# Taking beta1 h from the transposed h on chip in an edge-gated graph layer

## The chip, the cores and the metric

The kernel runs on one core of one Trainium2 chip. The metric is the device time of one launch in microseconds (us), and the number quoted is the median of several launches. The engines are TensorE (PE, with its weight loads shown apart as PEld), VectorE (DVE), ScalarE (ACT), GpSimd (POOL) and SyncE (SP). SP, ACT and POOL issue transfers (DMAs), each from a queue of its own.

## What is computed

`x` holds 16 batches of 1024 nodes with 256 features in fp32; `adj` is a 1024 x 1024 matrix of which only about 0.9% (with the diagonal) is not zero. With h = x:

```python
pre_u = jnp.einsum('bud,dk->buk', h_t, W1[:d])
pre_v = jnp.einsum('bvd,dk->bvk', h_t, W1[d:])
hidden = relu(pre_u[:, :, None, :] + pre_v[:, None, :, :] + b1)
S = sigmoid(jnp.einsum('buvk,ko->buvo', hidden, W2)[..., 0] + b2[0])
a_t = jnp.einsum('buv,bud->bvd', S * A_a, h_t)
m_t = jnp.einsum('uv,bud->bvd', A_m, h_t) * h_t
z_t = beta1 * h_t + beta2 * (jnp.einsum('bvd,de->bve', a_t, Wa) + ba) + beta3 * (jnp.einsum('bvd,de->bve', m_t, Wm) + bm)
```

The last line is the one that matters here: every output row is beta1 times its own h plus two products with 256 x 256 weights.

## The kernel before

**Tables and blocks.** The 16 batches form four groups of four (`GB`). Each group has a table in device memory, one row for each node: 1024 values of pre_u and the 1024 values of h of its four batches, 8 KB in all. A block is one group with one tile of 128 target nodes, so there are 32 blocks. Their order is a list, `order`: group 0 with tiles 0 to 5, group 1 with tiles 0 to 5, group 0 with tiles 6 and 7, group 1 with tiles 6 and 7, then groups 2 and 3 with all eight tiles each. Block 24 is thus the first of the last group, and block 31 the last of all.

**Steps.** A block has ten steps, 320 in all; a step handles 128 edge slots. In each step:

- POOL gathers 128 table rows (1 MB) into one of eight buffers `fetched` (L518);
- PE expands pre_v of the targets to the edge slots (`pc`, L615, two products of 512 columns), and DVE adds it to the gathered pre_u (L648);
- DVE takes relu, multiplies by W2 and sums, once for each of four batches (L656), and ACT makes the sigmoid (L659) and scales the left-hand matrices (L661);
- PE sums the gathered h rows into the targets (`acc`, L673), after which the buffer is free for another gather.

The engines' order is written out by hand. The loop over steps issues `expand(n + 2)`, then `products(n, ...)`, then `add(n + 1)` and `gate(n)`; so the product of a step is issued two steps ahead of its use. `after(step, f)` puts a piece of work off to the end of a later step. All engines take their own instructions in this order.

**What is made beside the steps, inside `products`.** `halves` computes pre_v of the next block from its transposed h (`hT`, L445). `rows` computes pre_u rows of a later group, in half-rows of eight PE instructions, and stores them in the table; the steps at which this runs stand in `plan`. `turn_over` transposes the sums (L691), ACT copies them to `LT` (L694), and DVE multiplies the part that needs it by the transposed h (`times_h`, L705). In blocks 0 to 10 the edge lists of four later target tiles are also made, mostly by small DVE instructions that fill gaps (`lists`).

**The end of a block (`block_end`).** It runs within the following block, in steps 4 to 7 (from step 10 of the kernel on). It makes z in two halves of two batches each. For each half PE adds the bias row and eight products of 256 columns (L722) in PSUM, ACT copies the sum to a part of `LT` that is no longer needed (L736), and one step later DVE computes hb = hb * beta1 + z (L737); SP stores it to `out` (L739). hb is a tile `h_blk` (four buffers) into which SP loads h of the two batches from the table, in steps 5 and 7 of the block itself (L921). In the last group's second halves DVE isn't used: PE adds beta1 times the identity (`be1_eye`) times hb to the sum (L726), and ACT copies it to hb (L728).

**The transposed h.** A tile `hT` of 512 KB holds the transposed h of one block. Eight such tiles circulate in a list `hT_free`, three more from step 110 on; a few loads use two other tiles (`hta`). `drop_hT` returns a tile to the list. Before the change this happens after the second `times_h` of the block, at step 3 of the following block. The loads of `hT` are issued by SP at the steps in `plan`: for groups 2 and 3 in step 56 + 10 i and 136 + 10 i, for the second loads of group 1 in step 37 + 10 i.

Of the kernel before, what the change touches and what calls it, by code (L numbers as in the profile page):

```python
# [7 lines left out]
FP = mybir.dt.float32  # L8
# [3 lines left out]
ALU = mybir.AluOpType  # L12
AX = mybir.AxisListType
P = 128
# [3 lines left out]
def kernel(  # L18
# [42 lines left out]
    nc = tc.nc  # L61
    B, N, D = x.shape
    NT = N // P
    DC = D // P
    GB = 4
    NG = B // GB
    GD = GB * D
    W = 64
    NW = P // W
    TW = 5  # L70
    E = TW * P
# [9 lines left out]
    const = ctx.enter_context(tc.tile_pool(name="const", bufs=1))  # L81
# [94 lines left out]
    ident = fixed([P, P], "ident")  # L176
# [32 lines left out]
    big = main.enter_context(tc.tile_pool(name="big", bufs=2))  # L209
# [3 lines left out]
    lst = ExitStack()  # L213
    lists_done = lst.close
    lst = lst.enter_context(tc.tile_pool(name="lst", bufs=1))
# [26 lines left out]
    def lists(vt):  # L242
# [49 lines left out]
        first = R[:, 1:2]  # L292
# [34 lines left out]
        nc.vector.tensor_tensor(thr[:, vt:vt + 1], last, none, ALU.add)  # L327
        yield "op"
        RR = lst.tile([P, NW, RC], FP, name="RR", bufs=2)
        few = lst.tile([P, E], mybir.dt.uint8, name="few", bufs=2)  # L330
        yield "slot"
        for w, mine in enumerate((soon, late)):
            nc.vector.tensor_scalar(RR[:, w, :], R, mine, None, ALU.mult)
# [68 lines left out]
    def after(step, f):  # L402
        due.setdefault(step, []).append(f)
# [19 lines left out]
    def drop_hT(k):  # L423
        del hTs[k]
        if k in hT_of:
            hT_free.append(hT_of.pop(k))
# [77 lines left out]
            pass  # L504

    T = TW * NW

    BS = NG * NT

# [89 lines left out]
    def scale_late():  # L599
        nc.vector.tensor_scalar(ba_b, ba_b, be2, None, ALU.mult)  # L600
        nc.vector.scalar_tensor_tensor(bias, bias, be3, ba_b, ALU.mult, ALU.add)
        spread(bias_p, bias)
        nc.vector.tensor_scalar(w_a, w_a, be2, None, ALU.mult)
        nc.vector.tensor_scalar(w_m, w_m, be3, None, ALU.mult)
        hT_free.append(spare_)

# [19 lines left out]

    running = []
    be1_eye = []  # L630

    def piece_of(r, n):

# [49 lines left out]
    def turn_over(k, w, q, step):  # L683
        if w == 0 and q == 0:
            LTs[k] = one.tile([P, GB, 2, DC, P], FP, name="LT")
        LT = LTs[k]
        pt = small("pt").rearrange("p (r k c v) -> p r k c v", r=2, c=DC, v=V)
        ev = evs.pop(q)
        for i in range(4):
            r, c = divmod(i, DC)  # L690
            nc.tensor.transpose(pt[:, r, :, c, :], ev[:, r, c * P:(c + 1) * P], ident)  # L691
        v = slice(w * W + q * U, w * W + (q + 1) * U)
        r = (w * W + q * U) // V
        nc.scalar.copy(LT.rearrange("p b k c (r v) -> p r (b k c) v", v=V)[:, r:r + 2],  # L694
                       pt.rearrange("p r k c v -> p r (k c) v"))
        apart = k == BS - 1 and w == NW - 1
        if not apart:
            if not q:
                return
            v = slice(w * W, (w + 1) * W)  # L700

        def times_h():
            m = LT.rearrange("p (b two) k c n -> p b (two k c) n", two=2)[:, :, DC:3 * DC, v]
            h = hTs[order[k]].rearrange("p (b two) c n -> p b (two c) n", two=2)[:, :, :, v]
            nc.vector.tensor_tensor(m, m, h, ALU.mult)  # L705
            if w == NW - 1 and q == 1:
                drop_hT(order[k])
        after(step + (1 if k == BS - 1 or w else 2), times_h)

    def block_end(k):  # L710

        g, vt = order[k]
        hb = hbs[k]
        for h in range(2):
            for i, wt in ((1, w_a), (0, w_m)):
                step = yield
                if i:
                    pz = small("pz")
                    add_row(pz, bias_p)
                for bb in range(2):  # L720
                    for c in range(DC):
                        nc.tensor.matmul(pz[:, bb * D:(bb + 1) * D], LTs[k][:, 2 * h + bb, i if bb else 1 - i, c, :], wt[:, c, :],  # L722
                                         start=False, stop=(i == 0 and c == DC - 1), skip_group_check=True)
            if h == 1 and g == NG - 1:
                for bb in range(2):
                    nc.tensor.matmul(pz[:, bb * D:(bb + 1) * D], be1_eye[0], hb[h][:, bb, :], start=False, stop=True,  # L726
                                     skip_group_check=True)
                nc.scalar.copy(hb[h], pz.rearrange("p (b d) -> p b d", b=2))  # L728
                b = g * GB + 2 * h
                after(step + 2, lambda hb=hb[h], b=b: nc.sync.dma_start(  # L730
                    out[b:b + 2, vt * P:(vt + 1) * P, :].rearrange("b p d -> p b d"), hb))
                continue
            z = pz.rearrange("p (b d) -> p b d", b=2)
            if step >= ROOM:
                z = LTs[k][:, 2 * h].rearrange("p k c n -> p (k c n)").rearrange("p (b d) -> p b d", b=2)
                nc.scalar.copy(z, pz.rearrange("p (b d) -> p b d", b=2))  # L736
            after(step + 1, lambda hb=hb[h], z=z: nc.vector.scalar_tensor_tensor(hb, hb, be1, z, ALU.mult, ALU.add))  # L737
            b = g * GB + 2 * h
            after(step + 2, lambda hb=hb[h], b=b: nc.sync.dma_start(  # L739
                out[b:b + 2, vt * P:(vt + 1) * P, :].rearrange("b p d -> p b d"), hb))  # L740
        del hbs[k], LTs[k]

# [42 lines left out]
    def plan(blocks, ns):  # L787

        for k, (load, *pieces) in zip(blocks, ns):
            loads[load] = k  # L790
            at.update((n, k) for n in pieces)

    plan(turn[NT:], ((1, 2, 4), (2, 8, 9), (5, 12, 18), (10, 19, 22), (20, 28, 29), (23, 32, 38), (30, 39, 42), (40, 48, 49)))
    for g, first in ((2, 60), (3, 140)):
        plan([(g, vt) for vt in range(NT)], ((first - 4 + 10 * i, first + 8 + 10 * i, first + 12 + 10 * i)
                                             for i in range(NT)))
    plan([(1, vt) for vt in range(FIRST)], [(37 + 10 * i,) for i in range(FIRST)])
    plan([(g, vt) for g in range(2) for vt in range(FIRST, NT)], ((103,), (113,), (125,), (133,)))
    begun = set(turn[:NT])
    end = parts = piece = last = None  # L800
# [81 lines left out]
    for n in range(total + 2):  # L882
# [26 lines left out]
        if n == 1:  # L909
# [3 lines left out]
            be2 = load_rows(beta2, 1, "be2", nc.sync)  # L913
            be3 = load_rows(beta3, 1, "be3", nc.sync)
            after(10, scale_late)
        if s in (5, 7) and k < BS - 1:
            h = s // 7
            hb = big.tile([P, 2, D], FP, name="h_blk", bufs=4)
            hbs.setdefault(k, []).append(hb)
            g, vt = order[k]  # L920
            nc.sync.dma_start(hb.rearrange("p b d -> p (b d)"),  # L921
                              table[g][vt * P:(vt + 1) * P, GD + 2 * h * D:GD + (2 * h + 2) * D])
# [14 lines left out]
        if n == LISTS:  # L937
            assert not running and all(next(x, None) is None for x in made)
            lists_done()
            more = main.enter_context(tc.tile_pool(name="more", bufs=1))  # L940
            hT_free.extend(hT_places(more, MORE, NH))
            be1_eye.append(more.tile([P, P], FP, name="be1_eye"))
            nc.vector.tensor_scalar(be1_eye[0], ident, be1, None, ALU.mult)
        if n == 120:
            nc.gpsimd.partition_all_reduce(longest, rest, P, bass_isa.ReduceOp.max)
            after(n + 12, count_rest)
# [115 lines left out]
```

## Time and profile before

| quantity | value |
|---|---|
| median of 3 launches | 1077.57 us (1075.32 to 1079.38) |
| profiled launch, own time | 1082.24 us |
| its span, first to last instruction | 1080.4 us |
| PE busy (7673 matmuls) | 1020.1 us |
| DVE busy | 1017.6 us |
| ACT busy | 862.6 us |
| POOL busy | 459.3 us |
| bytes moved by DMA | 394.56 MB, mean 365 GB/s |

The page lists instructions in groups: the line of the source, the engine, the operation, what is written and read, how many there are; then the time in which at least one of them ran, the mean of one in ns, and the idle time of the engine ahead of them with what ended it. The groups that belong to the end of a block, from the list with shapes kept apart:

```profile
L722 PE MATMUL misc<-w_m,LT 128*128 128x256 f32 x496 | 117.3, 379 | 0.0
...
L737 DVE SCALAR_TENSOR_TENSOR h_blk<-h_blk,be,LT 128x512 f32<-128x512 f32 x55 | 40.9, 744 | 0.0
...
L736 ACT COPY LT<-misc 128x512 f32<-128x512 f32 x55 | 32.0, 582 | 29.1 <-PE misc L722 25.6 <-PE pc L615 1.4 <-issue 1.0
...
L726 PE MATMUL misc<-h_blk,be_eye 128*128 128x256 f32 x28 | 7.2, 379 | 0.0
```

PSUM tiles of 512 columns that change owners often carry the name `misc` there. Matmuls overlap, so the mean of one (379 ns) is longer than the time from one to the next (117.3 us for 496 of them). And the transfers:

```profile
h_blk<-table SPq DMA_DIRECT2D x62, 256.0 KB
out_dram<-h_blk SPq DMA_DIRECT2D x62, 256.0 KB
hT<-in_xT_dram SPq DMA_DIRECT2D x28, 512.0 KB
```

In views of windows each row gives a stretch of time, its length, the busy time and number of instructions of PE, PEld, DVE, ACT and POOL, the granted clock of PE, the busy share of the DMA engines and what they moved. In the chain of waits and in the timeline each row begins with the start and the length in us.

### The profile page before, as it was taken

To read this page: it belongs to the slowest core of one execution; us is meant where nothing else is said; L and a number is where in the kernel's file an instruction comes from. 1 tells how busy PE (TensorE), PEld (TensorE's weight loads), DVE (VectorE), ACT (ScalarE), POOL (GpSimd) and SP (SyncE) were. 2 spreads that over 40 slices of the span, in tenths; PEclk is the share of its full clock that TensorE was granted. 3 is DMA by queue.
4 is the path that set the end of the run, shared out by engine and by line. 5 is a ranking of instruction groups with operands and counts; after the bars stand their busy time and mean duration, and the time that the engine had idled before them with its cause. 6 is when DMAs were issued, how large, how long until landed. Compare 5 with 4: busy or idle time off the path is not lost.

```text
span 1080.4 us, 24120 instructions
## 1 busy us (share of the span) xinstructions
PE 1020.1 (94%) x7673; PEld 731.3 (68%) x7673; DVE 1017.6 (94%) x3481; ACT 862.6 (80%) x2616; POOL 459.3 (43%) x456
## 2 busy tenths in 40 slices
PE   7777999999999999999999999999999999999996
PEld 6654676776666776677777767777766667666654
DVE  8687999998999999999999999999999999999993
ACT  3246787788888887898888888889889889999983
POOL 2666676555257334553333334333333333333330
PEclk9989999999999999999999999999999999999999
DMA  9999899999999999999999999999999999999991
GB/s 283 327 340 385 313 339 381 362 382 378 403 352 371 408 381 385 379 403 395 404 393 399 412 384 392 408 396 389 381 361 370 369 348 368 365 381 369 365 341 44
DMA packets 147752, 394.56 MB, mean 365 GB/s; under 512 B 18224, under 2 KB 94512, under 8 KB 111408
## 3 DMA queue, kind: packets, MB, share of 16 engines
q0 software_dynamic: 50544, 301.16, 70.9%
q1 hardware_dynamic: 83776, 78.66, 22.9%
q10 hardware_dynamic: 13296, 13.11, 3.5%
q8 instruction: 63, 1.03, 0.4%
q14 instruction: 73, 0.60, 0.1%
HBM read 396.93 MB, written 50.33 MB: 414 GB/s over the span
## 4 chain that ended last, share of the span: by engine, by line
PE 40%; DVE 34%; issue 10%; ACT 8%; DMA 5%; POOL 2%; another core or an unknown queue 0%; POOLq 0%; DVEq 0%; ACTq 0%
DVE fetched L656 16%; DVE fetched L648 12%; PE acc L673 10%; PE misc L722 10%; PE misc L445 9%; PE pc L615 7%; DMA fetched<-table,uidx 3%; PE misc L691 2%; ACT left L661 2%; DVE LT L705 1%; ACT X L489 1%; PE misc L449 1%; DVE low L484 1%; DVE h_blk L737 1%; DMA hT__635<-in_xT_dram 1%
## 5 line engine op out<-in xcount | busy, mean ns | idle before, releaser
L518 POOL DMA_INDIRECT fetched<-table,uidx x320 | 339.4, 1061 | 529.0 <-PE acc L673 389.0
L656 DVE SCALAR_TENSOR_TENSOR fetched<-fetched,w_b 128x256 f32<-128x256 f32 x1280 | 478.0, 419 | 0.0
L648 DVE TENSOR_TENSOR fetched<-fetched,pc 128x1024 f32<-128x1024 f32 x320 | 387.7, 1212 | 29.9 <-PE pc L615 19.4
L661 ACT ACTIVATE left<-left,gt 128x32 f32<-128x32 f32 (+1 forms) x1280 | 299.6, 305 | 10.4
L673 PE MATMUL acc<-fetched,left 128*32 128x256 f32 x4096 | 273.4, 385 | 6.3 <-ACT gt L659 3.7
L615 PE MATMUL pc<-X,mark 128*128 128x512 f32 x640 | 243.7, 462 | 10.9 <-DVE fetched L648 9.3
L673 PEld LDWEIGHTS acc<-fetched,left 128*32 128x32 f32 x4096 | 127.6, 109 | 112.1 <-issue 29.1
L615 PEld LDWEIGHTS pc<-X,mark 128*128 128x128 f32 x640 | 105.4, 189 | 88.9 <-issue 41.6
L659 ACT ACTIVATE gt<-sc,b_b 128x4 f32<-128x4 f32 x320 | 95.9, 300 | 46.7 <-DVE fetched L656 37.5
L722 PE MATMUL misc<-w_m,LT 128*128 128x256 f32 x496 | 117.3, 379 | 0.0
L722 PE MATMUL misc<-w_a,LT 128*128 128x256 f32 x496 | 117.2, 379 | 0.0
L445 PE MATMUL misc<-w_v,hT 128*128 128x256 f32 x448 | 107.6, 383 | 0.0
L722 PEld LDWEIGHTS misc<-w_a,LT 128*128 128x128 f32 x496 | 93.8, 189 | 15.3 <-issue 0.4
L722 PEld LDWEIGHTS misc<-w_m,LT 128*128 128x128 f32 x496 | 93.8, 190 | 15.1
L625 ACT ACTIVATE left<-onehot,val 128x64 f32<-128x64 bf16 (+1 forms) x320 | 102.9, 322 | 0.0
L385 POOL DMA_INDIRECT val<-in_adjT_dram,vidx x80 | 87.2, 1090 | 34.4 <-issue 20.4
L656 DVE DVE_READ_ACCUMULATOR fetched<-fetched,w_b 128x1 f32 x1280 | 100.7, 79 | 0.0
L691 PE MATMUL misc<-ident,ev 128*128 128x128 f32 x512 | 79.5, 278 | 18.5 <-issue 7.0
L445 PEld LDWEIGHTS misc<-w_v,hT 128*128 128x128 f32 x448 | 86.4, 193 | 14.3
L691 PEld LDWEIGHTS misc<-ident,ev 128*128 128x128 f32 x512 | 60.7, 141 | 45.7 <-ACT ev L681 15.2
L482 ACT CAST X<-misc 128x512 fp32r<-128x512 f32 x64 | 37.1, 580 | 55.2 <-PE misc L445 48.0
L445 PE MATMUL misc<-w_u,hT 128*128 128x256 f32 x320 | 76.6, 386 | 4.0 <-issue 3.8
(185 smaller groups left out, 1011.3 us busy)
## 6 DMA issues: line engine op xcount, KB each, us to landing
h_blk<-table SPq DMA_DIRECT2D x62, 256.0 KB
out_dram<-h_blk SPq DMA_DIRECT2D x62, 256.0 KB
hT<-in_xT_dram SPq DMA_DIRECT2D x28, 512.0 KB
table<-in_x_dram ACTq DMA_DIRECT2D x24, 512.0 KB
table<-tab SPq DMA_DIRECT2D x48, 256.0 KB
fetched<-table,uidx POOLq DMA_INDIRECT x320
table<-in_x_dram SPq DMA_DIRECT2D x8, 512.0 KB
table<-fetched SPq DMA_DIRECT2D x8, 512.0 KB
```

Of the source, the lines that this page charges most:

```text
L385: nc.gpsimd.indirect_dma_start(out=val[:, i, j:j + 1], out_offset=None, in_=adj_flat, in_offset=bass.IndirectOffsetOnAxis(ap=vidx[:, i, j: ...
L445: nc.tensor.matmul(p[:, bb * D:(bb + 1) * D], hT[:, 2 * h + bb, i, :], wt[:, i, :], start=(i == 0 and not begun), stop=(i == DC - 1), skip ...
L518: nc.gpsimd.indirect_dma_start(out=fetched[at_slot[n]], out_offset=None, in_=table[g], in_offset=bass.IndirectOffsetOnAxis(ap=uidx[:, vt * ...
L615: nc.tensor.matmul(pcs[n][:, c], marks[n // TW][:, j * P:(j + 1) * P], cuts[k][:, w, c], start=True, stop=True)
L625: nc.scalar.activation(lefts[n][:, :m, 1::GB, :], onehot[:, i, o:o + m, :].unsqueeze(2).to_broadcast([P, m, GB // 2, V]), AF.Copy, scale=v ...
L648: nc.vector.tensor_tensor(t, t, pcs.pop(n), ALU.add)
L656: nc.vector.scalar_tensor_tensor(t[:, b, :], t[:, b, :], 0.0, w2_b, ALU.max, ALU.mult, accum_out=sc[:, b:b + 1])
L659: nc.scalar.activation(gt, sc, AF.Sigmoid, bias=b2_b)
L661: nc.scalar.activation(lefts[n][:, :m, 2 * b, :], lefts[n][:, :m, 1 + b // 2 * GB, :], AF.Copy, scale=gt[:, b:b + 1])
L673: nc.tensor.matmul(accs[h][b * 2 * V:(b + 1) * 2 * V, r, :], left[:, i, 2 * b - b % 2:2 * b - b % 2 + 2].rearrange("p k v -> p (k v)"), f[ ...
L691: nc.tensor.transpose(pt[:, r, :, c, :], ev[:, r, c * P:(c + 1) * P], ident)
L722: nc.tensor.matmul(pz[:, bb * D:(bb + 1) * D], LTs[k][:, 2 * h + bb, i if bb else 1 - i, c, :], wt[:, c, :], start=False, stop=(i == 0 and ...
```

## The change

In blocks 0 to 9 (both halves) and in the second halves of blocks 24 to 30, beta1 h is added on PE from the transposed h that is on chip: for each batch and each half of the features, the 128 x 128 tile of `hT` is the weight and `be1_eye` the moving operand, which gives beta1 h untransposed, added into the same sum in PSUM. Those halves have no load of `h_blk` and no DVE instruction; ACT copies the finished sum to a fresh `h_blk` tile and SP stores it. So that `hT` is there, `drop_hT` moves behind the second half of `block_end` in these blocks (step 7 of the following block), and the loads of `hT` in groups 2 and 3, and the second loads of group 1, move two steps later; with those of groups 2 and 3 go the copies of h into the table, issued by ACT. `be1_eye` is made at step 10 and lies in another pool; to make room, `few` has one buffer in place of two.

```diff
-        few = lst.tile([P, E], mybir.dt.uint8, name="few", bufs=2)
+        few = lst.tile([P, E], mybir.dt.uint8, name="few", bufs=1)
...
+    BOTH, SECOND = range(10), range(24, 31)
...
+        be1_eye.append(const.tile([P, P], FP, name="be1_eye"))
+        nc.vector.tensor_scalar(be1_eye[0], ident, be1, None, ALU.mult)
...
+    def from_hT(k, h):
+        return k in BOTH or h == 1 and k in SECOND
...
-            if w == NW - 1 and q == 1:
+            if w == NW - 1 and q == 1 and not from_hT(k, 1):
                 drop_hT(order[k])
...
-            if h == 1 and g == NG - 1:
+            if from_hT(k, h):
                 for bb in range(2):
-                    nc.tensor.matmul(pz[:, bb * D:(bb + 1) * D], be1_eye[0], hb[h][:, bb, :], start=False, stop=True,
-                                     skip_group_check=True)
-                nc.scalar.copy(hb[h], pz.rearrange("p (b d) -> p b d", b=2))
+                    for c in range(DC):
+                        nc.tensor.matmul(pz[:, bb * D + c * P:bb * D + (c + 1) * P], hTs[order[k]][:, 2 * h + bb, c, :], be1_eye[0],
+                                         start=False, stop=True, skip_group_check=True)
+                if h == 1:
+                    drop_hT(order[k])
+                hb = big.tile([P, 2, D], FP, name="h_blk", bufs=4)
+                nc.scalar.copy(hb, pz.rearrange("p (b d) -> p b d", b=2))
...
-        plan([(g, vt) for vt in range(NT)], ((first - 4 + 10 * i, first + 8 + 10 * i, first + 12 + 10 * i)
+        plan([(g, vt) for vt in range(NT)], ((first - 2 + 10 * i, first + 8 + 10 * i, first + 12 + 10 * i)
                                              for i in range(NT)))
-    plan([(1, vt) for vt in range(FIRST)], [(37 + 10 * i,) for i in range(FIRST)])
+    plan([(1, vt) for vt in range(FIRST)], [(39 + 10 * i,) for i in range(FIRST)])
...
-        if s in (5, 7) and k < BS - 1:
+        if s in (5, 7) and k < BS - 1 and not from_hT(k, s // 7):
```

## What I expect

> **What bounds the kernel now.** I read the page's first two parts first: PE is busy 94% of the span, DVE 94%, ACT 80%, and the DMA row is at 9 tenths everywhere. Three resources look full, so the share over the span decides nothing. The question is which wait ends last in each stage. I therefore asked for the busy time in windows cut at the start of every tenth row-add (L648), one window per block of ten steps. The first ten windows below are blocks 1 to 10. The next two are blocks 12 to 21 and 25 to 29.
>
> ```profile
> core 0: us, PE busy (x) PEld busy (x) DVE busy (x) ACT busy (x) POOL busy (x), PEclk, DMA share, GB/s
> 100.50:140.80 40.30, 33.48 (x222) 23.31 (x224) 35.85 (x133) 27.51 (x83) 26.76 (x27) 0.92 0.91 315
> 140.80:177.30 36.50, 35.70 (x278) 25.89 (x271) 36.50 (x131) 28.70 (x87) 23.23 (x25) 1.00 1.02 373
> 177.30:212.50 35.20, 32.06 (x224) 23.52 (x222) 33.62 (x121) 27.33 (x83) 20.71 (x22) 1.00 1.01 367
> 212.50:243.50 31.00, 31.00 (x238) 23.03 (x237) 30.82 (x107) 24.70 (x75) 16.93 (x16) 1.00 1.02 377
> 243.50:279.50 36.00, 34.39 (x272) 23.58 (x270) 33.10 (x119) 29.77 (x93) 16.91 (x17) 1.00 1.03 386
> 279.50:313.00 33.50, 31.20 (x240) 22.00 (x238) 33.50 (x122) 26.33 (x82) 13.21 (x15) 1.00 0.98 368
> 313.00:342.30 29.30, 28.03 (x196) 20.30 (x194) 29.30 (x98) 24.88 (x77) 20.28 (x18) 1.00 1.01 366
> 342.30:372.40 30.10, 29.66 (x227) 21.25 (x227) 29.05 (x97) 25.50 (x79) 13.25 (x13) 1.00 1.03 406
> 372.40:407.10 34.70, 33.15 (x256) 23.74 (x258) 33.45 (x122) 29.14 (x91) 10.86 (x10) 1.00 1.01 387
> 407.10:441.10 34.00, 33.48 (x275) 23.89 (x267) 33.88 (x120) 27.99 (x85) 14.04 (x16) 1.00 1.03 390
> ...
> 471.40:773.80 302.40, 300.55 (x2321) 218.64 (x2320) 290.42 (x955) 263.27 (x810) 107.35 (x101) 1.00 1.02 397
> 862.50:1003.60 141.10, 137.41 (x1087) 97.64 (x1089) 141.10 (x472) 127.59 (x395) 50.11 (x49) 1.00 0.97 363
> ```
>
> Blocks 25 to 29 are bound by DVE: 141.10 of 141.10 us. Blocks 12 to 21 are bound by PE: 300.55 of 302.40, 30.2 us a block. Blocks 1 to 10 are mixed. DVE is full in blocks 2, 6, 7 and 10 (in three of them list-making runs beside the block); PE is full in block 4. DMA is busy in all of them, and yet it hardly ends a wait: of DVE's waits in the next fence 19.4 us end with a product of PE, 2.7 us with a gather.
>
> ```profile
> DVE fetched L648 <- PE pc L615: 19.4, 21, 2.0
> ...
> DVE fetched L648 <- DMA fetched<-table,uidx: 2.7, 1, 2.7
> ```
>
> That one gather is in the chain of waits, just ahead of block 1, and a 4.24 us hole without a named cause follows it:
>
> ```profile
> 87.20 10.01 DMA fetched<-table,uidx
> ...
> 103.16 4.24 another core or an unknown queue
> ```
>
> **What the Trainium skill says.** "Perfetto Trace Analysis", section "Optimization Strategy", says that a kernel can have several regimes with different most-contended engines; the windows agree. "DMA: Bandwidth & Descriptors", section "Issuing engines are not separate DMA queues", says that DMAs of all issuing engines interleave on the same 16 DMA engines, so SP's loads of h slow POOL's gathers; a store issue on SP that takes 16.97 us (L739 at 366.76 in the timeline) agrees that the queues are full. "TensorE: Matmul & The Clock Gate", section "Back-to-back issue gap", gives about half the gap for 128 columns that it gives for 256; the trace has the durations for this type below.
>
> **The change, part by part.**
>
> *New matmuls.* Each converted half-block gets four products of 128 columns with 128x128 weights; the fp32 product is two instructions (L722 has 496 for each weight tile, 31 blocks x 16, twice the source's count). The nearest row is the transposes of L691, also 128 columns on 128x128 weights: four loads take 0.57 us and one lasts 141 ns in the mean, so they follow each other by (570-141)/3 = 143 ns as merged, and by 109 ns where they run back to back (start to start at 744.18 us). L722, of 256 columns, has eight loads in 1.72 us: (1720-190)/7 = 219 ns. I take 110 ns: 8 x 0.110 = 0.88 us a half. Ends: 0.86 (exactly half of L722) and 1.15 (143 ns). Per block of the first ten that is +1.76 us of PE (1.7 to 2.3), 17.6 us in all.
>
> *DVE.* L737 disappears from those halves: 20 x 744 ns = 14.9 us, 1.49 a block. ACT's copy out of PSUM stays (582 ns before, 566 after, to another tile), but it now waits for 0.88 us more of PE; behind it on ACT stands the gate of the same step. be1_eye moves from step 110 to step 10: 0.28 us of DVE either way.
>
> *Loads.* 20 + 7 loads of 256 KB go, 7.1 of 394.6 MB. What hides this part is that gathers land before they are needed; only around 97 us does one end DVE's wait. The two loads for block 0 (issued at 86.31 and just after) stand ahead of that gather: 0.524 MB at the 397 GB/s of the window 66 to 100 us is 1.3 us. I take -1.3; ends 0 and -2.7 (the whole wait).
>
> *Last group.* Four products of 128 columns (0.88 us) replace two of 256 (28 instructions of L726 for 7 halves: 4 x 216 ns = 0.86). DVE has nothing removed, and DVE sets these blocks: 0. If DVE had slack, PE's 137.4 of 141.1 would leave 0.7 us a block.
>
> *Buffers and moved steps.* `few` in one buffer makes the copy of the third list wait for the index stores of the second. The updates of their semaphores end at about 50.8 us, the copy starts at 52.52: hidden by 1.7 us; without that cover the first gathers, queued behind it on POOL, start that much later. The tiles of transposed h come free at step 7 of the next block, not at 3, and the loads go two steps later, past a store of out on SP; the copies of h into the table go with them on ACT (0.56 us of issue each, unchanged). At steps 98 and 108 the only free tile is the one that PE read a step before, so SP waits there for that product, with stores of out and of table rows queued behind it; the gathers that read those rows start at step 152, and the first reader of a moved load comes ten steps after it, some 30 us: 0.
>
> *The sum for blocks 1 to 10.* What PE needs is calibrated on blocks 12 to 21: 30.2 us with two half-rows (L445, 8 x 0.216 = 1.73 each), so about 26.7 without. The plan puts 3, 3, 3, 3, 0, 1, 2, 2, 2, 2 half-rows into blocks 1 to 10, and the lists add about 1 us in blocks 1, 2, 5, 6, 9, 10 and 2 in block 3 (18 small products at 112 ns a list). PE needs 32.8, 33.0, 33.9, 31.9, 27.6, 29.5, 30.1, 30.1, 31.0, 31.2. DVE needs its busy time. The larger of the two, block by block, sums to 332.4 us, against 340.6 measured; the other 8.2 are single waits such as the hole at 103. With PE +1.76 and DVE -1.49 the larger values are 34.6, 35.0, 35.7, 33.7, 31.6, 32.0, 31.9, 31.9, 32.8, 33.0, sum 332.2. Blocks 1, 2, 5, 6, 9 and 10 win 0.7 to 1.5 us each, 3, 4, 7 and 8 lose 1.8 each: what DVE gives is taken by PE. So -0.2, and with the start -1.5. The profiled execution took 1082.24 us (span 1080.4 and 1.8 around it): 1080.7. Against the median of the runs, 1077.57, the same change gives 1076.
>
> **The rivals.** *PE absorbs it all.* The spans of PE in blocks 1 to 10 leave 340.6 - 311.1 = 29.5 us above its need. The product runs two steps ahead of its add, so a late PE can catch up over a block's border. Then the blocks that DVE binds keep their 1.49 (six blocks, 8.9), the four others neither win nor lose, and the start gives 1.3: -10, 1067. For: PE's weight loads are busy only two thirds of these windows. Against: 10 of the 29.5 us lie in block 1 ahead of the new work.
>
> *PE becomes the bound.* The new products stand in steps 5 and 7, where PE already has the four products of the block end. The add of each step needs its product in time, and at some steps it has nothing to spare: in the timeline at 368.42 the product's pair starts, 0.73 us long, and the add that reads it starts at 369.19.
>
> ```profile
> 368.42 0.73 PE L615 MATMUL pc<-X,mark 128*128 128x512 f32 x2
> ...
> 369.19 1.22 DVE L648 TENSOR_TENSOR fetched<-fetched,pc 128x1024 f32<-128x1024 f32 x1
> ```
>
> From the point where less than 1.76 us is to spare after step 7, each block pays the new work as DVE idle time. With six such blocks (3, 4, 7, 8, 9, 10) 10.6 us are paid, the four others win back about 3, and the start 1.3: +6.3, 1084. For: PE's later half-rows in the blocks without lists. Against: DVE itself comes 1.49 earlier only if PE lets it.
>
> *It doesn't do what it says:* the later loads of transposed h arrive late and PE waits in L445. Ten steps of cover speak against it; I give it 0.03, inside the slower case.
>
> **How the numbers follow.** Balance, as summed: 0.45, 1070 to 1081. PE absorbs: 0.35, 1062 to 1070. PE bound: 0.20, 1081 to 1089. Two runs of this kernel differ by up to 0.4%, so about 0.5% (1072.2 to 1083.0) can be told from no change. Of the balance case a tenth falls below that: faster 0.38, same 0.43, slower 0.19. The forecast is 1076. The range of 1065 to 1084 leaves out the far end of both rivals; the balance case alone has 1070 to 1081.
>
> **What would show it.** PE: 160 more instructions of about 0.11 us in blocks 1 to 10, and in those windows PE full and DVE with idle time in front of L648 that ends with L615. DVE: 35 rows of L737 left. Blocks with lists shorter, blocks 3, 4, 7 and 8 longer by up to 1.8. Blocks 25 to 29 at 28.2 us as before. The gather wait at 97 us shorter. I am wrong if blocks 3, 4, 7 and 8 don't get longer, if the time per new half is far from 0.88 us, or if the last group moves.

## The result, and the profile after

The changed kernel is slower: 1089.41 us, median of four runs (1088.33 to 1094.45), against 1078.25 us for four runs of the kernel before; the ratio is 1.0117, 95% interval 1.0079 to 1.0155. The forecast was 1076, its range 1065 to 1084. The profiled execution took 1089.14 us, its span is 1086.9.

The windows of the changed kernel, again cut at every tenth row-add (now L654): blocks 1 to 13 singly (5 and 6 are left out), then 14 to 21, then 25 to 29.

```profile
core 0: us, PE busy (x) PEld busy (x) DVE busy (x) ACT busy (x) POOL busy (x), PEclk, DMA share, GB/s
98.30:134.10 35.80, 32.02 (x215) 23.00 (x214) 34.58 (x132) 24.21 (x74) 25.31 (x25) 0.95 0.93 333
134.10:170.80 36.70, 36.70 (x282) 28.10 (x284) 35.26 (x127) 30.50 (x92) 24.52 (x26) 1.00 1.01 364
170.80:204.90 34.10, 32.72 (x257) 24.42 (x250) 32.10 (x119) 25.18 (x79) 19.82 (x21) 1.00 0.99 347
204.90:239.60 34.70, 34.43 (x264) 25.98 (x264) 29.71 (x105) 27.00 (x83) 18.37 (x19) 1.00 0.98 349
...
306.90:336.90 30.00, 29.93 (x240) 22.03 (x238) 28.32 (x98) 24.48 (x78) 20.54 (x19) 1.00 0.98 354
336.90:368.80 31.90, 31.83 (x249) 23.68 (x248) 27.84 (x93) 26.30 (x82) 12.53 (x12) 1.00 1.03 375
368.80:403.10 34.30, 33.53 (x258) 24.80 (x258) 32.20 (x120) 28.07 (x85) 10.21 (x10) 1.00 0.97 361
403.10:437.10 34.00, 34.00 (x266) 26.00 (x265) 32.37 (x118) 27.72 (x84) 13.08 (x15) 1.00 1.00 363
437.10:467.30 30.20, 30.13 (x235) 21.91 (x233) 29.17 (x97) 26.39 (x82) 22.02 (x20) 1.00 1.01 369
467.30:499.70 32.40, 32.33 (x261) 23.14 (x263) 29.16 (x96) 28.25 (x88) 10.81 (x11) 1.00 1.03 410
499.70:537.70 38.00, 29.81 (x206) 21.49 (x199) 29.55 (x99) 24.17 (x74) 10.81 (x10) 0.91 0.91 330
537.70:779.10 241.40, 240.82 (x1859) 175.32 (x1858) 232.40 (x762) 210.91 (x649) 83.29 (x80) 1.00 1.02 396
867.60:1008.60 141.00, 137.42 (x1105) 98.15 (x1107) 141.00 (x472) 127.62 (x396) 50.35 (x49) 1.00 0.95 352
```

In blocks 1 to 10 PE is now full, or nearly, where DVE was, and DVE has idle time everywhere. Yet these ten windows add up to 338.8 us, against 340.6 before: in this pair of profiles the balance of the ten blocks seems to come out. That is an accident of the profile before, as later profiles show: there the ten blocks of the kernel before take 332.1 us (f3) and, with one load moved, 332.8 (g2), and those of the changed kernel 338.7 (f4). The largest part of the difference is block 1, 40.3 us long in the first profile, with the 4.24 us hole in it, and 35.9 in f3. The last row, of blocks that VectorE binds, is unchanged. In this pair the time was lost in two windows without any new product: block 12 (32.4, before 30.0) and block 13 (38.0, before 30.7), and there is 1.4 us more behind the last window. Three waits of the changed kernel, summed over its whole span:

```profile
engine line waited for: us in total, times, longest us
...
DVE fetched L654 <- PE pc L618: 38.1, 31, 6.9
...
DVE fetched L654 <- DMA fetched<-table,uidx: 9.9, 10, 2.4
...
PE misc L445 <- DMA hT<-in_xT_dram: 8.1, 1, 8.1
```

VectorE's wait for products has doubled (19.4 before), its wait for gathers has grown from 2.7 to 9.9 (in f3, a second profile of the kernel before, it is 7.8), and a single wait of 8.1 us in block 13 isn't in the profile before: PE stands in L445, the half-products of the next block, until a transposed h has landed. SP's timeline of those blocks shows the load: it is issued at 480.76, and the trace has it landed at 513.2, 32.5 us later.

```profile
start us, us, engine line op out<-in xcount [idle before <-releaser]
...
462.38 0.38 SPq L434 DMA_DIRECT2D hT<-in_xT_dram  x1
467.41 0.39 SPq L749 DMA_DIRECT2D out_dram<-h_blk  x1
469.00 11.71 SPq L465 DMA_DIRECT2D table<-tab  x2
480.76 0.43 SPq L434 DMA_DIRECT2D hT<-in_xT_dram  x1
```

The load at 462.38 is a moved one (block 22, step 118 in place of 116). The load at 480.76 isn't moved (block 14, step 125, first read in step 131). Its distance from the moved one has shrunk: 18.4 us here, 27.7 in the profile before (issues at 456.42 and 484.07). That made the first theory.

### The profile page after: what moved, and what is told of

It is laid out like the page before. It is cut to its first block, busy times and chain, and to the rows that moved or that the text cites. A ratio compares the mean times of both kernels' runs of the same rounds, so it can differ in the third digit from the quotient of the medians.

```text
span 1086.9 us, 24447 instructions
## 1 busy us (share of the span) xinstructions
PE 1033.2 (95%) x7861; PEld 750.9 (69%) x7861; DVE 1007.0 (93%) x3461; ACT 861.7 (79%) x2616; POOL 451.4 (42%) x456
## 4 chain that ended last, share of the span: by engine, by line
PE 48%; DVE 21%; DMA 12%; ACT 9%; issue 7%; SPq 1%; POOL 1%; ACTq 0%; POOLq 0%; DVEq 0%
PE misc L728 12%; PE misc L445 12%; PE acc L679 11%; DVE fetched L662 10%; DVE fetched L654 8%; PE pc L618 7%; DMA fetched<-table,uidx 4%; DMA hT<-in_xT_dram 3%; ACT left L667 2%; PE misc L697 2%; PE misc L449 2%; DMA val<-in_adjT_dram,vidx 1%; ACT X L489 1%; DMA table<-in_x_dram 1%; PE misc L733 1%
## 5 line engine op out<-in xcount | busy, mean ns | idle before, releaser
L519 POOL DMA_INDIRECT fetched<-table,uidx x320 | 333.1, 1041 | 541.6 <-PE acc L679 411.5
L654 DVE TENSOR_TENSOR fetched<-fetched,pc 128x1024 f32<-128x1024 f32 x320 | 387.7, 1212 | 49.6 <-PE pc L618 38.1
L679 PE MATMUL acc<-fetched,left 128*32 128x256 f32 x4096 | 270.0, 384 | 4.7 <-ACT left L667 4.5
L618 PE MATMUL pc<-X,mark 128*128 128x512 f32 x640 | 240.8, 458 | 11.8 <-DVE fetched L654 11.8
L618 PEld LDWEIGHTS pc<-X,mark 128*128 128x128 f32 x640 | 103.6, 190 | 86.3 <-issue 39.5
L445 PE MATMUL misc<-w_v,hT 128*128 128x256 f32 x448 | 108.4, 386 | 8.1 <-DMA hT<-in_xT_dram 8.1
L445 PEld LDWEIGHTS misc<-w_v,hT 128*128 128x128 f32 x448 | 86.6, 193 | 22.7 <-DMA hT<-in_xT_dram 8.5
L700 ACT COPY LT<-misc 128x512 f32<-128x512 f32 x128 | 73.0, 571 | 3.3 <-PE misc L697 3.3
```

Of the source, the lines that this page charges most:

```text
L445: nc.tensor.matmul(p[:, bb * D:(bb + 1) * D], hT[:, 2 * h + bb, i, :], wt[:, i, :], start=(i == 0 and not begun), stop=(i == DC - 1), skip ...
L519: nc.gpsimd.indirect_dma_start(out=fetched[at_slot[n]], out_offset=None, in_=table[g], in_offset=bass.IndirectOffsetOnAxis(ap=uidx[:, vt * ...
L618: nc.tensor.matmul(pcs[n][:, c], marks[n // TW][:, j * P:(j + 1) * P], cuts[k][:, w, c], start=True, stop=True)
L654: nc.vector.tensor_tensor(t, t, pcs.pop(n), ALU.add)
L679: nc.tensor.matmul(accs[h][b * 2 * V:(b + 1) * 2 * V, r, :], left[:, i, 2 * b - b % 2:2 * b - b % 2 + 2].rearrange("p k v -> p (k v)"), f[ ...
```

## First experiments: the moved loads

Theory A blamed the moved steps, Theory B the price of the matmuls. Ratios below are against runs of the kernel before on the same chip in the same group of runs, with 95% intervals.

**e1_two_back.**

```
-first - 2 + 10 * i
+first - (4 if i in (6, 7) and g == 2 else 2) + 10 * i
```

> The changed kernel with two of the moved loads put back: transposed h of blocks 22 and 23 (and the copies of h issued with them) at steps 116 and 126 as before, not 118 and 128. Theory A (the loss of some 10 us in blocks 12 and 13 comes from these two megabyte-sized steps being issued two steps later, in a stretch where the DMA engines are full, so that the load of block 14's transposed h issued at step 125 lands late): the 8.1 us wait of PE in L445 goes, block 13 takes about 30.5 us instead of 38.0, the time is 1079 to 1082. Rival B (the loss is the price of the new matmuls, and the wait only shows where it comes out): no change, 1088 to 1091. Rival C (loads of h dropped earlier let the gathers run further ahead and fill the DMA queues): also no change, 1086 to 1091.

**e2_shift_alone**, the edit made in the kernel before:

```
-first - 4 + 10 * i        -37 + 10 * i
+first - 2 + 10 * i        +39 + 10 * i
```

> The kernel before with nothing but the moved steps: loads of transposed h of groups 1 to 3 two steps later, loads of h and adds on VectorE as before. Theory A: a wait of PE in L445 near block 13 appears and the time rises by 6 to 11 us, to 1084 to 1089. Rivals B and C: 1077 to 1080, as before.

**e3_no_second.**

```
-BOTH, SECOND = range(10), range(24, 31)
+BOTH, SECOND = range(10), ()
```

> The changed kernel with the last group left as before: no product from transposed h in blocks 24 to 30. My prediction held the last group at 0: then 1088 to 1091, and groups 3's block windows stay at 28.2 us. If the seven freed additions of VectorE were worth 744 ns each it would be 5 us slower, 1094; if the seven products of PE cost their 0.88 us each it would be 6 us faster, 1083.

**e4_at_119.**

```
-((103,), (113,), (125,), (133,))
+((103,), (113,), (119,), (133,))
```

> The changed kernel with only the load of block 14's transposed h issued at step 119 instead of 125, all else left. Theory A in its narrow form (one late load stops PE, and all else in the stretch has slack): the wait in L445 goes and the time is 1079 to 1082. Theory A in its wide form (the DMA engines owe more bytes than they can move by block 13, so that something else comes late instead, a gather or a load of h): the wait moves to another line and the time stays above 1085. Rival B: 1088 to 1091.

Measured: e1 1.0103 (1.0042 to 1.0163), e2 1.0000 (0.9972 to 1.0029), e3 1.0115 (1.0062 to 1.0168), e4 1.0114 (1.0052 to 1.0175). By these numbers Theory A lost: two moves undone win nothing, and all moves alone cost nothing. But there is a catch in the same results. In this group of runs the kernel before itself took 1089.52 us, 11 us more than in the first, and no profile of the group has the wait of L445 for block 14's load. So the group says that the loss is there without that wait; it can't say what the wait costs where it occurs. Where the loss stands instead can be seen in its profiles: blocks 1 to 10 take 343.4 us in e2, which has no product, and 352.5, 352.2 and 347.2 in e1, e3 and e4, which have them.

The edit of e3 did more than its expectation says. In the kernel before, the second half of a last-group block had its own product from a loaded h; that went too, so the edit gave VectorE one addition a block. The windows show it: blocks 25 to 29 take 28.9 us each with it, VectorE full in them; in the changed kernel it is 28.2, VectorE just as full.

```profile
878.10:1022.50 144.40, 138.37 (x1082) 94.95 (x1081) 144.40 (x477) 128.69 (x397) 50.95 (x50) 1.00 0.96 357
```

That is 0.68 us per addition of 744 ns, the one place in this case where an addition's price is met almost in full.

## Relief and price apart

**f1_relief_alone** takes the new products out, those of the last group too, and so leaves beta1 h out of those halves; **f2_price_alone** puts loads and additions of the ten blocks back beside the products (beta1 h is added twice there). f3 and f4 are the two kernels unchanged.

```
f1  -nc.tensor.matmul(pz[:, ...], hTs[order[k]][:, 2 * h + bb, c, :], be1_eye[0], ...)
f2  -if s in (5, 7) and k < BS - 1 and not from_hT(k, s // 7):
    +if s in (5, 7) and k < BS - 1 and not (k in SECOND and from_hT(k, s // 7)):
     ...
     if h == 1:
         drop_hT(order[k])
    +if g == NG - 1:
         ...
         continue
     z = pz.rearrange("p (b d) -> p b d", b=2)
```

> The changed kernel without the new matmuls: loads of h and additions dropped, moved steps kept, and beta1 h left out of the output of the halves concerned. The first runs took the blame from the moved steps, so now: Theory B (in blocks 1 to 11 TensorE binds as often as VectorE, and it pays the new matmuls in full while the additions that VectorE loses are worth little): the relief alone is worth 0 to -5 us against the kernel before, the ratio is 0.995 to 1.0. Theory D (the relief is worth its 15 us as I counted, and something else than the matmuls takes it back): ratio 0.985 to 0.99. If the relief itself were the harm (gathers that run ahead, or the output tile that comes late from its rotation): above 1.003.

> The changed kernel with the loads of h and VectorE's additions of the first ten blocks back as before, so that TensorE's new matmuls come on top (beta1 h is added twice there). Theory B: the price is 11 to 18 us, ratio 1.010 to 1.017, about that of the whole change. My prediction's sum (VectorE binds half of the blocks, TensorE's matmuls lie beside it there): 8 to 10 us, ratio 1.008 to 1.009. If the matmuls are not the cause: ratio 0.997 to 1.003.

> The kernel before, unchanged, for a profile of it on the chip of these runs: ratio 1.0. If the gaps of this kernel lie in the same steps on every chip, blocks 4 and 7 take 31 and 29.3 us as in the first profile; if they differ by chip, their lengths do too.

> The changed kernel, unchanged, for a profile of it on the chip of these runs: ratio 1.008 to 1.015. If the 8 us wait for block 14's transposed h belongs to the change, L445 waits for it again in block 13; Theory B: block 13 takes some 30 us here and the loss sits in blocks 4, 7, 8 and 11, with PE busy through them.

Measured: f1 0.9976 (0.9958 to 0.9993), f2 1.0143 (1.0092 to 1.0195), f3 0.9996, f4 1.0127 (1.0092 to 1.0163); the kernel before took 1076.7 us. So, beside everything else of the change, the products cost 1.0127 - 0.9976 = 1.5%, 16.3 us. I had 17.6 us of PE work for them in the ten blocks. (The seven halves of the last group are in this difference too, but blocks 25 to 29 take 141.0 us in all four profiles.) Theory B's numbers were met.

The ten blocks as one window each, columns as above, for f3 (kernel before), f1 (relief alone), f2 (price alone) and f4 (changed kernel):

```profile
98.06:430.15 332.09, 318.01 (x2398) 229.56 (x2396) 328.42 (x1157) 271.60 (x824) 178.67 (x175) 0.99 1.02 382
```

```profile
99.08:424.14 325.06, 315.70 (x2387) 229.18 (x2389) 314.88 (x1139) 270.41 (x822) 173.94 (x175) 0.99 1.01 373
```

```profile
99.67:443.98 344.31, 333.55 (x2536) 247.61 (x2539) 329.45 (x1157) 270.51 (x822) 177.65 (x174) 0.99 1.00 366
```

```profile
99.05:437.71 338.66, 330.14 (x2520) 246.03 (x2519) 317.00 (x1137) 268.54 (x816) 172.44 (x175) 0.99 0.99 357
```

In these windows the products cost 12.2 us with the additions there (f3 to f2) and 13.6 without (f1 to f4); the relief is worth 7.0 us without products (f3 to f1) and 5.6 with them (f2 to f4). Both together, f3 to f4, cost 6.6 us. VectorE's idle time grows from 3.7 to 21.7 us, PE's shrinks from 14.1 to 8.5.

VectorE's waits in the windows of blocks 1 to 10, in the same order:

```profile
DVE fetched L648 <- PE pc L615: 0.6, 2, 0.4
```

```profile
DVE fetched L654 <- PE pc L618: 9.7, 8, 2.4
```

```profile
DVE fetched L654 <- PE pc L618: 8.1, 8, 2.5
```

```profile
DVE fetched L654 <- PE pc L618: 18.1, 15, 3.4
```

VectorE gave up 14.9 us of additions and waits 9 us longer for products even if PE has nothing new to do (f1); with the products it waits 18. Where it waits can be read from the starts of the adds. Summed over the ten blocks, the two steps in which the additions stood (from the add of step 7 to that of step 8, and from 9 to the next block's first) shrank from 68.6 us (f3) to 55.2 (f1), nearly all of the 14.9. The next step, from a block's first add to its second, grew from 29.4 to 35.9 (f1) and 41.4 (f4). VectorE comes early to the border of a block, and there it stands until PE has the product of the second step. The timelines of f4 show one such place, the first step of block 4; first PE, then VectorE:

```profile
204.25 0.72 PE L733 MATMUL misc<-be_eye,hT 128*128 128x128 f32 x5
204.73 0.71 PE L618 MATMUL pc<-X,mark 128*128 128x512 f32 x2
205.28 1.22 PE L341 MATMUL misc<-RR,made 128*128 128x58 f32 x10
206.33 1.95 PE L445 MATMUL misc<-w_u,hT__1793 128*128 128x256 f32 x8
208.56 0.66 PE L697 MATMUL misc<-ident,ev 128*128 128x128 f32 x4 [0.27 <-ACT L L345]
209.14 1.93 PE L679 MATMUL acc<-fetched,left 128*32 128x256 f32 x32
211.01 0.73 PE L618 MATMUL pc<-X,mark 128*128 128x512 f32 x2
```

```profile
205.75 1.21 DVE L654 TENSOR_TENSOR fetched<-fetched,pc 128x1024 f32<-128x1024 f32 x1
...
211.78 1.22 DVE L654 TENSOR_TENSOR fetched<-fetched,pc 128x1024 f32<-128x1024 f32 x1 [3.43 <-PE pc L618]
```

Between the pairs of L618 at 204.73 and 211.01, PE has one pause of 0.27 us. The new matmuls, small products of a list, a half-row, transposes and the sums stand one behind another in the order of the program, and the add that needs the second product waits 3.43 us.

The four profiles bring a second result, on the first theory. The wait in block 13 is in all of them, in the kernel before too. f3's line:

```profile
PE misc L445 <- DMA hT<-in_xT_dram: 7.8, 1, 7.8
```

So that wait doesn't belong to the change alone; the first profile of the kernel before happened to be without it.

## My sum's winners, and the wait in block 13

**g1_lists** (products in blocks 1, 2, 5, 6, 9, 10), **g2_before_119** and **g3_after_119** (block 14's load at step 119), **g4_two_119**:

```
g1  -BOTH, SECOND = range(10), range(24, 31)
    +BOTH, SECOND = (0, 1, 4, 5, 8, 9), range(24, 31)
g2, g3, g4  -((103,), (113,), (125,), (133,))
            +((103,), (113,), (119,), (133,))
g4  also BOTH = (4, 5)
```

> The changed kernel with the products only in blocks 1, 2, 5, 6, 9 and 10, those that my sum had as winners because VectorE makes lists there; blocks 3, 4, 7 and 8 get loads of h and additions back. My sum: 7.3 us faster than the kernel before in these blocks, ratio about 0.993. Theory B (TensorE's new work is paid there too, and the relief of VectorE is worth about as much): ratio 0.999 to 1.005, so most of the change's loss goes with blocks 4 and 8 and the rest stays.

> The kernel before with the load of block 14's transposed h at step 119 instead of 125. In the last profiles the 8 to 10 us wait of L445 in block 13 stood in the kernel before and in the changed one alike, with 32 us from issue to landing in both. If it is a cost of both and not of the change: here L445 doesn't wait, block 13 takes some 30 us, ratio 0.990 to 0.995 where the kernel before shows the wait, 1.0 where it doesn't. If the wait only moves to the next transfer (a full DMA queue that owes the bytes anyway): ratio 1.0 and the 8 us in another line.

> The changed kernel with the same move of that one load. Same two readings: if the wait is common to both kernels this is 1.003 to 1.006 against the kernel before (its 1.012 less the wait), and the distance to the kernel before with the same move stays 12 to 14 us; if the wait was a part of what the change costs, that distance shrinks to 3 to 6 us.

> A version meant to beat both: products only in blocks 5 and 6, the one pair that was shorter in the changed kernel (by 1.5 us) than in the kernel before, the last group as changed, and the load at step 119. Theory B with the wait as a cost of both kernels: ratio 0.988 to 0.994, at or 1.5 us below the kernel before with the move alone. If blocks 5 and 6 win nothing: equal to it.

Measured, against 1077.05 us: g1 1.0079 (1.0054 to 1.0105), g2 0.9995 (0.9971 to 1.0019), g3 1.0134 (1.0050 to 1.0217), g4 1.0052 (1.0032 to 1.0072). g1 fell outside both expectations, on the slow side: a choice of blocks that I had as 7 us faster costs 8.5. g4 didn't beat the kernel before.

g2's profile has no wait in block 13, and that execution was the fastest of its twelve (1070.59), but their median is the kernel before's. In g3 and g4 the load is there in time and PE stands elsewhere. g3's waits:

```profile
ACT tab L461 <- DMA table<-tab: 10.4, 2, 9.7
PE misc L697 <- ACT tab L461: 9.2, 2, 8.5
```

The half-row of the table is copied from PSUM into a tile of which there is only one for each half; its last store hasn't landed; ACT waits, and the next transposes of PE wait for the PSUM tile that ACT hasn't read. In these two profiles the next transfer of SP's queue is late in place of the load, the second reading of g2's expectation. In g2's own profile nothing took the wait's place (block 13 takes 30.3 us), and yet its median stayed: how often the kernel before has the wait, and what it costs there, stays open.

## Work at other steps

Here I believed that TensorE binds a block's turn and has room in steps 1 to 3 (the phase theory, against a total theory: TensorE has too little left over the whole block). **h2_early_products** issues f1's missing products at steps 1 and 2 into a PSUM tile without a reader, **h3** and **h4** move the half-rows there, **h5** gives three loads to POOL's queue:

```
h2  +if s in (1, 2) and 0 < k < BS and k - 1 in BOTH:
    +    spent = small("spent")
     ...
    +            nc.tensor.matmul(spent[:, ...], hTs[order[k - 1]][:, 2 * (s - 1) + bb, c, :], be1_eye[0], ...)
h3, h4  -first + 8 + 10 * i, first + 12 + 10 * i
        +first + 12 + 10 * i, first + 13 + 10 * i     (group 2; group 1's steps likewise)
h5  -load_hT(loads[n])
    +load_hT(loads[n], nc.gpsimd if n in (116, 125, 126) else nc.sync)
```

> The changed kernel with the eight new products of each of the first ten blocks issued at steps 1 and 2 of the next block in place of steps 5 and 7, into a tile of PSUM that nobody reads (beta1 h is left out of the output of those halves, and the last group has none). It has to be held against the run without any of the products (ratio 0.998) and the changed kernel (1.013). Phase theory: TensorE has room at steps 1 and 2, the price is under half of its 13 to 15 us: ratio 0.999 to 1.005. Total theory: the place doesn't matter, 1.010 to 1.015.

> The changed kernel with the half-rows of the table (1.7 us of TensorE each) moved from steps 8 and 9 of blocks 0 to 14 to steps 1, 2 and 3 of the blocks after. Phase theory: VectorE's idle time before the add of a block's second step (13 us in blocks 1 to 10 of the changed kernel, 0.5 in the one before) falls to under 5 us, the ratio to 1.003 to 1.008. Total theory: TensorE's work is the same, ratio 1.010 to 1.015.

> The kernel before with the same move of the half-rows. Its VectorE waits only some 2 us for products in blocks 1 to 10, so by the phase theory the move has little to win: ratio 0.996 to 1.002. By the total theory: 0.998 to 1.002. Slower than 1.004 would mean that steps 1 to 3 were full as well.

> The kernel before with three loads of transposed h (steps 116, 125 and 126) issued by POOL, on the gathers' queue, in place of SP. If the wait in block 13 is owed by SP's queue alone (small pieces beside the gathers' large ones): the load lands within 10 to 15 us, L445 doesn't wait, block 13 takes 30 us, ratio 0.991 to 0.996 on a chip where the kernel before shows the wait. If the DMA engines owe the bytes as a whole: a gather or a table store comes late instead, ratio 0.998 to 1.003.

Measured, against 1083.55 us: h2 1.0206 (1.0139 to 1.0274), h3 1.0247 (1.0181 to 1.0312), h4 1.0211 (1.0135 to 1.0287), h5 1.0007 (0.9984 to 1.0029). All three moves cost 22 us or more where the phase theory allowed 9 at most, so as I put it, it is wrong. The total theory fails too: h3 and h4 lie above its 1.015 and 1.002. But none of the three moved only what it was meant to. h4, the kernel before with other steps for the half-rows, waits for its own stores:

```profile
ACT tab L461 <- DMA table<-tab: 12.0, 2, 10.7
```

and h2's extra tile takes a turn in the two PSUM tiles that all small products share, so PE waits for ACT there (L862 is the moved product):

```profile
PE misc L862 <- ACT tab L461: 3.8, 6, 1.1
```

They show how little a step can be moved in this kernel, and don't settle where PE has room. h5's profile has no wait in block 13, and yet its median is the kernel before's. Since no profile of the kernel before was taken in this group, whether there was a wait to remove stays open.

## The remainder of the change

**i1_last_group** keeps everything of the change but the ten blocks' products: `BOTH = ()`. **i2_step_before** issues the products right behind the bias row:

```
     add_row(pz, bias_p)
    +for bb in range(2 * from_hT(k, h)):
    +    for c in range(DC):
    +        nc.tensor.matmul(pz[:, ...], hTs[order[k]][:, 2 * h + bb, c, :], be1_eye[0], start=False, stop=False, ...)
```

> The changed kernel with no product in the first ten blocks: their loads of h and additions as before, the last group, the moved steps and the single buffer as changed. If the loss belongs to the products of the ten blocks alone: ratio 0.998 to 1.002. If the remainder has a price of its own, as the run with products in two blocks only suggests (1.005 where a share of two in ten would be 1.003): 1.002 to 1.004.

> The changed kernel with the new products of a half issued one step earlier, right behind the bias row, in place of behind the products of the block end; same tile, same work, same output. If TensorE's lateness is a matter of its total in the block: ratio 1.011 to 1.015 as for the changed kernel. If it is the steps 7 to 0 that are late (there VectorE waited 17 of its 18 us in the changed kernel): a step of head start gives some of it back, 1.006 to 1.011.

Measured, against 1077.52 us: i1 1.0099 (1.0061 to 1.0138), i2 1.0133 (1.0080 to 1.0187). i2 says that a step's head start is worth nothing. i1 is the surprise of the study. The last group, the moved steps, the single buffer and the earlier identity, together and without a product in the ten blocks, cost 10.7 us (`hT` is also given back at step 3 there, as before); i1 misses both its expectations. Its runs spread from 1080.14 to 1093.36, and the profiled one is the slowest of them. Its waits:

```profile
PE misc L445 <- DMA hT<-in_xT_dram: 9.6, 1, 9.6
...
ACT tab L461 <- DMA table<-tab: 8.3, 2, 5.5
```

Block 13's wait is there, and a second one on SP's queue: 5.5 us at 189.5 us, a table store that holds up ACT and through it the transposes, five steps before the first moved load is due (step 39). Block 3 takes 40.5 us with it, 33.8 in f3. None of the four profiles of the f group, nor i2's or the changed kernel's first, has such a wait there; the most that ACT waits for a table store in any of them is 2.3 us (f2). So the 10.7 us can't be taken as a part of what the changed kernel loses.

## Why the prediction was wrong, point by point

- **The step that failed: what TensorE needs in blocks 1 to 10, and with it the sum, -0.2.** The sum took 311.1 us for PE, carried over from blocks 12 to 21, and read 29.5 us above it as room. The prediction's own windows have PE busy for 322.1 us in these blocks (34.39 in block 5, where the sum has 27.6), and f3's for 318.0. With the busy time in place of the need, the same rule, the larger of the two engines block by block, gives 331.2 before and 339.7 after: +8.6 from the prediction's own lines, where it had -0.2. Measured from f3 to f4: +6.6. I priced the products as if about half of them lay in PE's idle time, and of that there was less: 18.5 us in the first profile and 14.1 in f3, in place of 29.5.

| blocks 1 to 10, us against f3 | the sum's rule, with its need of PE | the same rule, with PE's busy time in f3 | measured |
|---|---|---|---|
| relief alone (f1) | -8.9 | -7.2 | -7.0 |
| price alone (f2) | +7.0 | +9.8 | +12.2 |
| both (f4) | -0.2 | +7.6 | +6.6 |

The two columns of the rule are estimates, worked out from the windows. Each kernel has one profile here. Why PE is busy for longer than the carried-over need wasn't worked out, nor is it shown that all this busy time is needed. Block by block the rule is coarser: blocks 4 and 8 got longer (by 3.9 and 2.2 us from f3 to f4), 3 and 7 hardly (0.3 and 0.7); of the winners only block 5 won (1.3), and 1, 2, 6, 9 and 10 stayed within 0.8. What the larger of two can't see is where in a block the time goes: VectorE's saving in steps 7 and 9 was in part waited off at the next block's first step.

- **The second step: "Buffers and moved steps", closed with "0".** Outside the ten blocks the changed kernel lost another 6.0 us from f3 to f4: 1.0 ahead of block 1, 4.0 in blocks 11 to 13, 1.1 behind the last window; for f1 it is 5.8, for f2 2.6. I held a load safe because "the first reader of a moved load comes ten steps after it, some 30 us", and never set that against the time such a load takes in this stretch: 27.4 us for the moved one at 462.38, which was in time for its reader, and 32.5 for the unmoved one behind it, which was not. Nor did I ask who waits for what is queued behind: of the table's stores I named only the gathers that read the rows much later, not the tile that the next half-row is copied into. The Trainium skill's "DMA: Bandwidth & Descriptors", section "Issuing engines are not separate DMA queues", on which the prediction drew, says that the DMAs of all engines interleave on the same 16 DMA engines; those two load times beside the gathers, and 7.0 us for a load issued while the gathers stood, agree. I used it for the gathers and not for SP's own loads.
- **Which part of the remainder costs it is open.** i1, which has the remainder without the ten blocks' products, measured +10.7 us (6.6 to 14.9), but its profile has a wait in block 3 that no profile of the f group has. For the moved steps: all eight profiles of kernels with them in the groups of f, g and i, and the first of the changed kernel, have a wait of 8 to 11 us on SP's queue in block 13; of the two profiles of the kernel before and g2's, one has it. Against: e2, the moved steps alone, at 1.0000, though in a group without that wait; none of the eight profiles of the groups of e and h has it, and six of these kernels have moved steps; and i1's 5.5 us wait, before any moved load. The single buffer and the last group were not run alone. The profile of the last group itself is unchanged (141.0 us for five blocks), and the end behind it is 1.1 to 1.4 us longer in the changed kernel's two profiles, for no cause that I found.
- **The ratios alone would mislead.** Beside the kernel before at 1 (i1 from another group of runs than the other three):

| | additions and loads kept | dropped |
|---|---|---|
| no products in the ten blocks | 1.0099 (i1) | 0.9976 (f1) |
| products | 1.0143 (f2) | 1.0127 (f4) |

  From these, relief would be worth 13 us without products and under 2 with them, and the ten blocks' part of the change only 3.0 us (i1 to f4, with some 5.6 either way). The windows have 7.0, 5.6 and 6.6. The 13 and the 3.0 rest on i1 and its extra wait; that each engine binds only when the other is relieved is not shown.
- **Right:** 0.88 us a half (the eight instructions of L733 start 112 ns apart in the median, 0.90 us); 20 additions gone (L747 has 35 left); VectorE idle ahead of the row-add on a product; the last group at 28.2 us.
- **The start:** -1.3 us isn't shown. The first add came 4.0 us earlier in the first pair and 1.3 later from f3 to f4.
- **The rivals:** "PE becomes the bound" describes what the waits show, and its +7.6 us for the ten blocks (10.6 less about 3) is near the 6.6 measured; six blocks paid 8 us of the 10.6 forecast. It had the remainder at 0 as well, so that its 1084 fell short. "PE absorbs it all" counted on the 29.5 us; and the part of them in block 1 is 7.5 by the prediction's own figures (40.3 less 32.8), not 10. The wait in L445, which I gave 0.03, did occur; the kernel before has it too in f3.

No version beat the kernel before by more than f1's 0.24%, which leaves the term out.

## What to carry to other kernels

Price new work on an engine against the time that the engine is busy in that same stage, not against a need carried over from another stage: here that is the difference between -0.2 and +8.6 us, from the same lines. Cover of so many microseconds is worth something only beside the time that the same transfer takes in the same stretch: read its landing there, and list every tile, not only every reader, that waits for what is queued behind it. Where two engines are both near full, run the four corners and compare the windows of the stage, not the whole time alone: a transfer of a full queue can come 8 us late in one execution and not in the next.

## What the hardware showed that I hadn't expected

A 512 KB load on SP's queue landed after 27.4 and 32.5 us in the stretch where gathers fill the DMA engines (410 GB/s), and after 7.0 us right behind the wait that had stopped the gathers (none was issued between 505.30 and 520.57). After that wait of 8.1 us the first eight instructions of L445 took 634 ns in the median, where others of the same shape take 379; the granted clock of that window is 0.91. The view of the tile of transposed h in the changed kernel, from 455 to 520 us, has the durations (ns, least/median/most) and the landings (us):

```profile
L445 PE MATMUL misc<-w_u,hT x32: 377/379/379, 465.6 to 518.9; 128*128 128x256 f32 x32
...
L445 PE MATMUL misc<-w_v,hT x8: 634/634/793, 513.3 to 516.4; 128*128 128x256 f32 x8
...
DMA to landing us min/median/max: 7.0/27.4/32.5
```

And the same kernel's median lay at 1077, 1083.6 and 1089.5 us in different groups of runs, about as far apart as the change moves it: only ratios within a group were used, but for i1 in the table of ratios.
